# Seven half-depth products for eight in Q, K and the experts' first layers, and an accumulating transfer in the softmax sums, in a fused attention and expert kernel

## The chip, the cores and the metric

The kernel runs on one core of one Trainium2 chip. All data are fp32; only the negated row maxima of the softmax go through TensorE in bf16, each split into three bf16 parts. The metric is the device time of one execution in microseconds (us).

Engines are named as in the profile: PE is TensorE's matmul stream, PEld its weight loads, DVE is VectorE, ACT is ScalarE, POOL is GpSimd, SP is SyncE, which here only starts DMAs.

## The reference, cut to what matters

```python
xn = (x - mean(x)) / sqrt(var(x) + 1e-5)            # x: (4, 2048, 512)
q, k, v = split(xn @ qkv_w.T + qkv_b)               # 16 heads of 32
a = softmax(q @ k.T / sqrt(32)) @ v
attn = a @ proj_w.T + proj_b
idx = top_k(x_in[:, 0, :] @ Wr + br, 2)             # of 8 experts; x_in is xn's first token
h = gelu(xn @ W1[idx] + b1[idx])                    # 512 -> 512
ffn = sum(h @ W2[idx] + b2[idx]) / 2
out = x + attn + ffn
```

Each of the four batch entries ("batches" below) uses its own two experts, over all 2048 tokens.

## The kernel before, in words

**Units.** Attention is cut into *units*: one batch `b`, one group `g` of four heads (128 rows of Q and K), one chunk `qc` of 512 queries, one tile `kt` of 128 keys. 16 units make a chunk, 4 chunks a group, 4 groups a batch: 1024 units, written out by hand in one long loop over `U`, which starts 22 units early (`-LEAD`) because the row maxima run ahead of the softmax.

In each unit PE does four `shift` matmuls (minus the row maximum, L544), then `score` (L552) and `score_max` (L534, for a unit 22 later) in turns; ACT does four exponentials (L664) into a tile `p` (one for each head); DVE takes four maxima (L670). In every even unit PE also does `weigh` (L564: weights times V, of two units), and DVE adds the result to `sacc` (L573). POOL adds the unit's `p` tile to `psum` in `add_weights` (L581 and L583): the first of these in a chunk at `kt` 1, the last at `kt` 15 (the very last chunk of all has none). At `kt` 4 or 5 of the next chunk `add_keys` (L589) multiplies `psum` by ones to get the row sums; DVE inverts them in four pieces (L684) and POOL divides (L635).

**Items.** Every other product is an *item* placed in an odd unit, at most one to a unit, after its scores: a tile of Q or K (`kps`, `qps`), of V (`vps`), of an expert's first layer (`w1`, written as `hps`), of its second (`w2`, `ops`), or of the output projection (`prps`). An item is one PSUM bank of 128x512 and 16 calls of `nc.tensor.matmul`: four depth slices of 128, each as four column strips of 32 (L403). The trace has two instructions for a call, so an item is 32. Q, K and `w1` items leave PSUM by one ACT operation that adds the bias (L415), or by one on DVE (L413) where a gelu runs in the same unit; `w2` items by one DVE operation (L458) onto a `row` tile.

**The planner.** `Plan` gives every item its unit (the *slot*): Q, K and V at fixed places, the projection and the experts' items in the order of two queues in what is left. There are 534 slots, 496 items, 34 slots left empty ("rests", at `kt` 5). `Plan.loads` then says after which unit each tile is fetched: 8 units ahead of its first use, or when a buffer of its tag comes free. DMAs are all started on SP's queue, in program order; stores wait for a unit or two in `later`.

**Buffers.** PSUM has eight banks, all of one tag, taken in turn: a tile takes the bank of the tile eight before it. A unit takes eight banks for scores and maxima, a ninth for `weigh` or for an item; the ninth takes the bank of its own unit's first score tile. `p` has four buffers: the exponentials of unit `U+4` overwrite the tile of unit `U`, so they wait for everyone who reads that tile, POOL among them.

**Other work.** For the next batch, group 1 takes the statistics (DVE), group 2 normalizes (ACT) and transposes (`turn`: PE, copied by DVE); the results go to `xn_dram` and come back as `xq` or `xf`. POOL also adds the bias to 64 `row` tiles (L690).

Of the kernel before, what the change touches and what calls it, by code (L numbers as in the profile page):

```python
# [17 lines left out]
P = 128  # L18
# [3 lines left out]
TOP_K = 2  # L22
# [4 lines left out]
AHEAD = 6  # L27
WARN = 4


class Plan:
# [6 lines left out]
    def __init__(self, B, DC, NCH, NT, TPC):  # L38
# [11 lines left out]
        for t in range(NT):  # L50
            fixed[slots[t]] = ("v", 0, t)
        for G in range(1, B * DC):
            b, g = divmod(G, DC)
            for c in range(NCH):
                if g:
                    at = [(G - 1) * self.per_group + 2 * (7 + 4 * c) + 1]
                    todo = [("k", b, g, c), ("q", b, g, c)]
                else:
                    at = [(G - 2) * self.per_group + 2 * (27 + (2 + TPC) * c) + 1]
                    todo = [("k", b, g, c), ("q", b, g, c)]  # L60
                    todo += [("v", b, c * TPC + i) for i in range(TPC)]
                for n, item in enumerate(todo):
                    fixed[at[0] + 2 * n] = item
# [8 lines left out]
        for b in range(1, B):  # L72
            q1 = (b - 1) * self.per_seq + self.per_group
            q2 = q1 + self.per_group
            for n in range(NT):
                self.extra.setdefault(q1 + 2 * (16 + n) + 1, []).append(("stats", b, n))
                at = q2 + 2 * (1 + n + n // TPC) + 1
                self.extra.setdefault(at, []).append(("normal", b, n))
                self.extra.setdefault(at + 2, []).append(("turn", b, n))
            self.extra.setdefault(q2 + 1, []).append(("root", b, 0))  # L80
            for c in range(NCH):
                self.first_load[("xf", (b, c))] = self.first_load[("xq", (b, c))] = (
                    q2 + 2 * (2 + (TPC + 1) * c + TPC - 1) + 1 + 2
                )

        ffn = []
        for b in range(B):
            t0 = slots[0] if b == 0 else self.first_load[("xf", (b, 0))] + WARN
            order = list(range(NCH))
            if b == B - 1:  # L90
                order[NCH - 2 :] = order[: NCH - 3 : -1]
            for c in order:
                part = [("w1", b, c, k, f) for k in range(TOP_K) for f in range(DC)]
                part += [("w2", b, c, k, i) for k in range(TOP_K) for i in range(TPC)]
                ffn.append((t0, part))
# [16 lines left out]
        for s in slots:  # L112
            if s in fixed:
                self.items[s] = [fixed.pop(s)]
                before = None
                continue
            curve = before is not None and before[0] == "w1" and before[4] == DC - 1
            before = None
            if s in rests:
                owed += share  # L120
                if owed > 0 and not curve:
                    owed -= 1
                    continue
            if not current:
                for queue in (proj, ffn):
                    if queue and queue[0][0] <= s:
                        current = queue.pop(0)[1]
                        break
            if current:
                before = current.pop(0)  # L130
                self.items[s] = [before]
# [5 lines left out]

        for s in slots:
            for it in self.items.get(s, []):
                for tag, key in self.needs(it):  # L140
                    self.uses.append((s, tag, key))
            for kind, b, n in self.extra.get(s, []):
                if kind in ("stats", "normal"):
                    self.uses.append((s, "xl", (kind, b, n // TPC)))
                elif kind == "turn":
                    self.uses.append((s, "xq", ("stage", b, n // TPC)))
# [9 lines left out]
    @staticmethod  # L156
    def needs(item):
        TPC = CH // P
        kind, b = item[:2]
        if kind in "kq":  # L160
            g, c = item[2:]
            return [("xq", (b, c)), ("w" + kind, g)]
        if kind == "v":
            return [("xq", (b, item[2] // TPC)), ("wb", ("v",))]
        if kind == "w1":
            c, k, f = item[2:]
            return [("xf", (b, c)), ("w1", (b, k, f))]
        if kind == "w2":
            c, k, i = item[2:]
            return [("wb", ("w2", b, k)), ("row", (b, c, i))]  # L170
        qc, i = item[2:]
        return [("xl", ("at", b, qc)), ("wb", ("proj",)), ("prow", (b, qc, i))]
# [22 lines left out]
def block_kernel(  # L195
# [44 lines left out]
    xn_dram, v_dram, att_dram, part_dram = {}, {}, {}, {}  # L240
    for b in range(B):
        for c in range(NCH):
            xn_dram[b, c] = tc.dram_tile([P, DC, CH], F32, name=f"xn_dram_{b}_{c}")
            v_dram[b, c] = tc.dram_tile([P, TPC, D], F32, name=f"v_dram_{b}_{c}")
            att_dram[b, c] = tc.dram_tile([P, DC, CH], F32, name=f"att_dram_{b}_{c}")
            for i in range(TPC):
                part_dram[b, c, i] = tc.dram_tile([P, D], F32, name=f"part_dram_{b}_{c}_{i}")


    BUFS = {"xq": 2, "xf": 1, "xl": 1, "wk": 1, "wq": 1, "v": 6, "w1": 4, "wb": 2, "row": 4,  # L250
            "prow": 2}
# [10 lines left out]

    def x_rows(b, c):
        return x[b, ts(c, CH), :].rearrange("(t p) d -> p t d", p=P)

    def load(tag, key):
        name = f"{tag}_" + "_".join(str(k) for k in (key if isinstance(key, tuple) else (key,)))
        shape = {"xq": [P, DC, CH], "xf": [P, DC, CH], "xl": [P, TPC, D], "wb": [P, DC, D],
                 "row": [P, D], "prow": [P, D]}.get(tag, [P, DC, P])
# [4 lines left out]
        if tag in ("xq", "xf"):  # L274
            nc.sync.dma_start(t, xn_dram[key])
        elif tag == "v":
            b, g, c = key
            nc.sync.dma_start(t, v_dram[b, c][:, :, ts(g, P)])
        elif tag == "xl" and key[0] == "at":
            nc.sync.dma_start(t, att_dram[key[1:]])  # L280
        elif tag == "xl":
            nc.sync.dma_start(t, x_rows(*key[1:]))
        elif tag in ("wq", "wk"):
            col = "qkv".index(tag[1]) * D + key * P
            nc.sync.dma_start(t, qkv_wT.rearrange("(c p) n -> p c n", p=P)[:, :, col : col + P])
        elif tag == "w1":
            b, k, f = key
            src = W1[ds(expert(b, k), 1)].rearrange("o (c p) f -> p (o c) f", p=P)
            nc.sync.dma_start(t, src[:, :, ts(f, P)])
# [7 lines left out]
        elif tag == "row":  # L297
            b, c, i = key
            nc.sync.dma_start(t, x[b, c * CH + i * P : c * CH + (i + 1) * P, :])
# [24 lines left out]
    for c, tag in enumerate(("xl", "xf", "h", "h")):  # L324
        t = stream.tile([P, TPC, D], F32, tag=tag, name=f"x_0_{c}", bufs=2 if tag == "h" else 1)
        x_first.append(t)
# [8 lines left out]
    for tag in ("wk", "wq"):  # L335
        load(tag, 0)
    nc.sync.dma_start(x_first[1], x_rows(0, 1))
    nc.sync.dma_start(bv_bc, v_b.to_broadcast([P, D]))
    for c in range(2, NCH):
        nc.sync.dma_start(x_first[c], x_rows(0, c))  # L340

# [92 lines left out]

    def dense(item, U, on_dve):
        kind, b = item[:2]
        tiles = [held[n] for n in plan.needs(item)]
        if kind in "kq":
            project_qk(kind, *item[1:], *tiles, on_dve=on_dve)
        elif kind == "v":  # L440
            project_v(*item[1:], *tiles, U)
        elif kind == "w1":
            c, k, f = item[2:]
            xn, w = tiles
            if f == 0:
                hT[k] = stream.tile([P, DC, CH], F32, tag="h", name=f"h_{b}_{c}_{k}", bufs=2)
            pp = bank(f"hps_{b}_{c}_{k}_{f}")
            product(pp, [(w[:, d, :], xn[:, d, :]) for d in range(DC)])
            with_bias(hT[k][:, f, :], pp, b1s[b, k][:, f : f + 1], on_dve)
            if f == DC - 1:  # L450
                at = U + 2 if U > 0 or U == -1 else U + 1
                curves[at] = hT[k]
        elif kind == "w2":
            c, k, i = item[2:]
            w, row = tiles
            pp = bank(f"ops_{b}_{c}_{k}_{i}")
            product(pp, [(hT[k][:, f, ts(i, P)], w[:, f, :]) for f in range(DC)])
            nc.vector.scalar_tensor_tensor(row, pp, 0.5, row, ALU.mult, ALU.add)  # L458
            if k == TOP_K - 1:
                later(U + 2, lambda: nc.sync.dma_start(part_dram[b, c, i], row))  # L460
# [42 lines left out]
    for c in range(NCH):  # L503
        xn = load("xq", ("stage", 0, c))
# [5 lines left out]
        for kind in "kq":  # L510
            project_qk(kind, 0, 0, c, xn, held["w" + kind, 0])
# [63 lines left out]
    def add_weights(u):  # L575
# [3 lines left out]
        if kt == 1:  # L579
            psums[b, g, qc] = pair.tile([P, GH, CH], F32, tag="psum", name=f"psum_{b}_{g}_{qc}")  # L580
            nc.gpsimd.tensor_tensor(psums[b, g, qc], pT[u - 1], pT[u], ALU.add)  # L581
        else:
# [56 lines left out]
    for s, tag, key in loads.get(-LEAD - 1, []):  # L639
        load(tag, key)  # L640
    sum_bias(*load_bias(0))
    row_ready = {}

    for U in range(-LEAD, plan.units):
# [59 lines left out]
        for step, sb, n in plan.extra.get(U, []):  # L704
            if step == "stats":
                if n == 0:
                    norms[sb] = stat_tiles(sb)
                stats(norms[sb][0], n, held["xl", ("stats", sb, n // TPC)][:, n % TPC, :])
            elif step == "root":
# [3 lines left out]
            else:  # L713
                c, i = divmod(n, TPC)
                xs = held["xq", ("stage", sb, c)]
# [11 lines left out]
        for s, tag, key in loads.get(U, []):  # L727
            t = load(tag, key)
            if tag == "row":
# [6 lines left out]
        for n, c in ((16, NCH - 1), (1, NCH - 2)):  # L736
            if U == plan.units - n:
                tags = ("xf", "xq") if c == NCH - 1 else ("xl", "xq")
                t, rows = (
                    stream.tile([P, TPC, D], F32, tag=tag, name=f"end_{tag}", bufs=BUFS[tag])  # L740
                    for tag in tags
# [81 lines left out]
```

## Time and profile before

| | |
|---|---|
| median of three runs | 5113.08 us (5110.4 to 5116.17) |
| the profiled execution | 5115.77 us, of which 5114.0 us from its first to its last instruction (the span) |
| PE busy | 5037.9 us, 99% |
| POOL busy | 4534.9 us, 89% |
| DVE busy | 3448.0 us, 67% |
| ACT busy | 2515.2 us, 49% |
| DMA | 342.30 MB, mean 67 GB/s; 19.5% of the 16 DMA engines' time |
| granted PE clock | 0.998 |

Busy time is the time in which at least one instruction of an engine runs. Matmuls overlap each other and their ends are modelled, so the mean length of one (595 ns in an item) isn't its share of PE's time: the chain of waits gives that, where 32 of them take 3.57 us. In a row of the costliest groups stand the line, the engine, the operation, output and inputs by tile name, the shape, the count, the busy time, the mean of one, and then the idle time of the engine ahead of them with what ended it.

### The profile page before, as it was taken

To read this page: it belongs to the slowest core of one execution; us is meant where nothing else is said; L and a number is where in the kernel's file an instruction comes from. 1 tells how busy PE (TensorE), PEld (TensorE's weight loads), DVE (VectorE), ACT (ScalarE), POOL (GpSimd) and SP (SyncE) were. 2 spreads that over 40 slices of the span, in tenths; PEclk is the share of its full clock that TensorE was granted. 3 is DMA by queue.
4 is the path that set the end of the run, shared out by engine and by line. 5 is a ranking of instruction groups with operands and counts; after the bars stand their busy time and mean duration, and the time that the engine had idled before them with its cause. 6 is when DMAs were issued, how large, how long until landed. Compare 5 with 4: busy or idle time off the path is not lost. (4 is left out here: it accounts for less than half of the span.)

```text
span 5114.0 us, 108163 instructions
## 1 busy us (share of the span) xinstructions
PE 5037.9 (99%) x46020; PEld 1763.7 (34%) x46020; DVE 3448.0 (67%) x5491; ACT 2515.2 (49%) x4576; POOL 4534.9 (89%) x1430
## 2 busy tenths in 40 slices
PE   8999999999999999999999999999999999999999
PEld 2333333333333333333333333333333333333332
DVE  5666676776676677766776667766667666666762
ACT  1455555444544545554445545554454455545453
POOL 0699998998999999989999999989999999999992
PEclk9999999999999999999999999999999999999999
DMA  4211112211222212211122121312012121111112
GB/s 165 69 49 51 57 65 91 77 53 40 67 70 78 77 55 73 95 64 46 63 89 72 49 79 59 100 67 85 32 51 85 57 98 34 48 62 33 47 37 87
DMA packets 221732, 342.30 MB, mean 67 GB/s; under 512 B 14396, under 2 KB 129084, under 8 KB 207040
## 3 DMA queue, kind: packets, MB, share of 16 engines
q1 hardware_dynamic: 221248, 335.38, 19.5%
q8 instruction: 361, 5.91, 0.5%
q14 instruction: 123, 1.01, 0.1%
HBM read 251.71 MB, written 83.62 MB: 66 GB/s over the span
## 5 line engine op out<-in xcount | busy, mean ns | idle before, releaser
L583 POOL TENSOR_TENSOR psum<-psum,p 128x2048 f32<-128x2048 f32 x882 | 4008.1, 4544 | 193.3 <-ACT p L664 152.7
L670 DVE TENSOR_REDUCE mx<-m 128x1 f32<-128x512 f32 x4096 | 2542.4, 683 | 1041.2 <-PE m L534 1040.6
L664 ACT ACTIVATE p<-s 128x512 f32<-128x512 f32 x4096 | 2117.1, 603 | 1817.2 <-PE m L534 1729.7
L552 PE MATMUL s<-qT,kT 32*128 32x512 f32 x8192 | 1917.1, 587 | 0.0
L534 PE MATMUL m<-kT,qT 32*128 32x512 f32 x8192 | 1900.1, 589 | 3.9 <-ACT h L415 2.4
L534 PEld LDWEIGHTS m<-kT,qT 32*128 32x128 f32 x8192 | 926.2, 184 | 317.0 <-issue 242.8
L564 PE MATMUL acc<-p,v 128*32 128x512 f32 x8192 | 989.6, 601 | 38.5 <-ACT p L664 38.5
L552 PEld LDWEIGHTS s<-qT,kT 32*128 32x128 f32 x8192 | 767.7, 185 | 22.6 <-issue 2.2
L564 PEld LDWEIGHTS acc<-p,v 128*32 128x32 f32 x8192 | 214.7, 109 | 737.8 <-ACT p L664 423.4
L403 PE MATMUL ops<-wb_w,h 128*32 128x512 f32 x4096 | 466.0, 595 | 0.9 <-ACT p L664 0.2
L403 PE MATMUL hps<-xf,w 128*32 128x512 f32 x4096 | 466.0, 595 | 0.8
L573 DVE TENSOR_TENSOR sacc<-acc,sacc 128x512 f32<-128x512 f32 x448 | 309.7, 691 | 149.2 <-PE acc L564 149.2
L544 PE MATMUL s<-negm,ones_b 32*128 32x512 bf16 x4096 | 404.8, 385 | 2.0 <-ACT p L664 1.8
L544 PEld LDWEIGHTS <-ones_b 32*128 32x128 bf16 x4096 | 103.0, 91 | 857.5 <-issue 857.5
L581 POOL TENSOR_TENSOR psum<-p,p 128x2048 f32<-128x2048 f32 x63 | 286.0, 4540 | 119.4 <-ACT p L664 119.4
L415 ACT ACTIVATE h<-hps,b 128x512 f32<-128x512 f32 x114 | 78.3, 687 | 354.6 <-PE hps L403 354.6
L684 DVE RECIPROCAL sums<-sums 128x128 f32<-128x128 f32 x252 | 237.3, 942 | 0.7 <-ACT sums L601 0.7
L403 PE MATMUL vps<-wb_v,xq 128*32 128x512 f32 x2048 | 233.0, 595 | 2.3 <-issue 2.1
L403 PEld LDWEIGHTS ops<-wb_w,h 128*32 128x32 f32 x4096 | 120.0, 109 | 308.4 <-issue 229.8
L403 PEld LDWEIGHTS hps<-xf,w 128*32 128x32 f32 x4096 | 120.0, 109 | 307.0 <-issue 232.1
L403 PE MATMUL kps<-xq,wk 128*32 128x512 f32 x1920 | 218.4, 595 | 0.3 <-ACT p L664 0.3
L403 PE MATMUL qps<-xq,wq 128*32 128x512 f32 x1920 | 218.4, 595 | 0.1
(89 smaller groups left out, 1711.7 us busy)
## 6 DMA issues: line engine op xcount, KB each, us to landing
xq<-xn_dram SPq DMA_DIRECT2D x64, 1024.0 KB, 5.7
w<-in_W_dram SPq DMA_DIRECT2D x128, 256.0 KB, 3.2
xn_dram<-xq_stage SPq DMA_DIRECT2D x16, 1024.0 KB, 5.8
v_dram<-v SPq DMA_DIRECT2D x64, 256.0 KB, 2.6
xf<-xn_dram SPq DMA_DIRECT2D x16, 1024.0 KB, 5.5
v<-v_dram SPq DMA_DIRECT2D x64, 256.0 KB, 3.6
wb_w<-in_W_dram SPq DMA_DIRECT2D x16, 1024.0 KB, 6.6
row<-in_x_dram SPq DMA_DIRECT2D x64, 256.0 KB, 5.4
```

The costliest lines, as they stand in the source:

```text
L403: nc.tensor.matmul(pp[rows_of(j), :], lhsT[:, rows_of(j)], rhs, start=(first and n == 0), stop=(last and n == len(terms) - 1),)
L415: nc.scalar.activation(dst, src, AF.Identity, bias=col)
L534: nc.tensor.matmul(t, qT[b, g, qc][r, ts(i, P)], kT[b, g, kc][r, :], start=True, stop=True)
L544: nc.tensor.matmul(tiles[j], ones_b[r, :], negm[b, g, qc][r, :], start=True, stop=False)
L552: nc.tensor.matmul(tiles[j], kT[b, g, kt // TPC][r, ts(kt % TPC, P)], qT[b, g, qc][r, :], start=False, stop=True,)
L564: nc.tensor.matmul(acc[r, :], held["v", (b, g, kt // TPC)][:, (kt + n) % TPC, r], pT[u + n][:, j, :], start=(n == 0), stop=(n == 1),)
L573: nc.vector.tensor_tensor(t, acc, t, ALU.add)
L581: nc.gpsimd.tensor_tensor(psums[b, g, qc], pT[u - 1], pT[u], ALU.add)
L583: nc.gpsimd.tensor_tensor(psums[b, g, qc], psums[b, g, qc], pT[u], ALU.add)
L664: nc.scalar.activation(pT[U][:, j, :], tiles[j], AF.Exp, scale=SCALE)
L670: nc.vector.tensor_reduce(dst, t, AX.X, ALU.max, negate=True)
L684: nc.vector.reciprocal(sums[before][:, q], sums[before][:, q])
```

## The change

**Seven products.** Take a product of 2x2 blocks, C = A B, where A has two row blocks (K and Q of one group, or two 128-wide blocks of an expert's first layer) and two depth halves of 256, and B has two depth halves and two token chunks of 512. The kernel before forms the four blocks of C from eight half-depth products (two to an item). The kernel after forms seven:

```
S1 = A21 + A22    S2 = S1 - A11    S3 = A11 - A21    S4 = A12 - S2
T1 = B12 - B11    T2 = B22 - T1    T3 = B22 - B12    T4 = B21 - T2
P1 = A11 B11   P2 = A12 B21   P3 = S4 B22   P4 = A22 T4   P5 = S1 T1   P6 = S2 T2   P7 = S3 T3
C11 = P1 + P2                 C12 = P1 + P6 + P5 + P3
C21 = P1 + P6 + P7 + P4       C22 = P1 + P6 + P7 + P5
```

- The products of one step `i` for two blocks of the same kind (two pairs of chunks for Q and K, two pairs of rows for `w1`) share a slot: two banks, eight calls of matmul each. Steps go in the order 1, 6, 7, 5, 3, 4, 2, and step 5 is split over two slots of one product each, so that 8 slots stay 8. V, `w2` and the projection are as before.
- Every product is added into the SBUF tiles of C by `combine`: P1 is copied by ACT (or DVE), each of the others is added by one DVE operation, P5 by two.
- The weight sums S are made on POOL in place: for Q and K once at the start, for each expert in four operations of 128x512 (`ws`). The token sums T are made on POOL for each pair of chunks in four operations of 128x1024 in four units running (`tx`). Sums go to DRAM (`wqk_dram`, `ws_dram`, `t_dram`), and every product fetches its two factors as tiles `wt` (128 or 256 KB) and `xt` (512 KB).
- Experts' items now go by pair of chunks and by expert, so the `row` of the first expert is stored and fetched again for the second. Q's and K's slots move: the eight of a group stand in units 23 to 39 of the group before it (step 5 at `kt` 13 and 15).
- The tokens of batch 0 stay in `p` buffers until V is done. `v` has 4 buffers and not 6.

**The accumulating transfer.** The addition of a chunk's last `p` tile (`kt` 15) to `psum` is not a POOL operation any more but a DMA that adds, started on POOL's queue.

The core of the diff (loads, the list of uses and the tail are left out, except for what is told above):

```diff
+STEPS = (1, 6, 7, 5, 3, 4, 2)
+STORED = 6
...
+        halves = [(i, h) for i in STEPS for h in (((0,), (1,)) if i == 5 else ((0, 1),))]
         for G in range(1, B * DC):
             b, g = divmod(G, DC)
...
+            first = (G - 1) * self.per_group
+            for n, (i, h) in enumerate(halves):
+                at = (11, 12, 13, 14, 15, 16, 17, 19) if g else (3, 4, 5, 6, 7, 8, 9, 11)
+                fixed[first + 2 * at[n] + 1] = ("qk", b, g, i, h)
...
+            for k in range(TOP_K):
+                at = q1 + 2 * ((3 if b == 1 else 63) + 5 * k) + 1
+                for n in range(4):
+                    self.extra.setdefault(at + n, []).append(("ws", b, (k, n)))
...
+            for p in range(NCH // 2):
+                at = q2 + 2 * (12 + 15 * p) + 1
+                for n in range(4):
+                    self.extra.setdefault(at + n, []).append(("tx", b, (p, n)))
...
+                for k in range(TOP_K):
+                    part = [("w1", b, p, k, i, h) for i, h in halves]
+                    part += [("w2", b, p, 2 * p + 1, k, i) for i in range(TPC)]
+                    rest = [("w2", b, p, 2 * p, k, i) for i in range(TPC)]
+                    ffn += [(t0, part), (t0, rest)] if b == B - 1 else [(t0, part + rest)]
...
-    BUFS = {"xq": 2, "xf": 1, "xl": 1, "wk": 1, "wq": 1, "v": 6, "w1": 4, "wb": 2, "row": 4,
-            "prow": 2}
+    BUFS = {"xq": 2, "xt": 4, "xl": 1, "wt": 4, "v": 4, "wb": 2, "row": 4, "prow": 2}
...
+    def combine(i, x, c, b1, b2, on_dve):
+
+        add = nc.vector.tensor_tensor
+        biased = nc.vector.scalar_tensor_tensor
+        if i == 1 and on_dve:
+            nc.vector.tensor_copy(c[0, 0], x)
+        elif i == 1:
+            nc.scalar.activation(c[0, 0], x, AF.Identity)
+        elif i == 6:
+            add(c[0, 1], x, c[0, 0], ALU.add)
+        elif i == 7:
+            add(c[1, 0], x, c[0, 1], ALU.add)
+        elif i == 5:
+            biased(c[1, 1], x, b2, c[1, 0], ALU.add, ALU.add)
+            add(c[0, 1], x, c[0, 1], ALU.add)
+        else:
+            at, b_ = {3: ((0, 1), b1), 4: ((1, 0), b2), 2: ((0, 0), b1)}[i]
+            biased(c[at], x, b_, c[at], ALU.add, ALU.add)
...
+    def token_blocks(t, n):
+
+        sub = nc.gpsimd.tensor_tensor
+        b11, b12, b21, b22 = t[0][:, :2], t[1][:, :2], t[0][:, 2:], t[1][:, 2:]
+        if n == 0:
+            sub(b11, b12, b11, ALU.subtract)
+        elif n == 1:
+            sub(b12, b22, b12, ALU.subtract)
+        elif n == 2:
+            sub(b22, b22, b11, ALU.subtract)
+        else:
+            sub(b21, b21, b22, ALU.subtract)
...
-        if kind in "kq":
-            project_qk(kind, *item[1:], *tiles, on_dve=on_dve)
+        if kind == "qk":
+            g, i, pairs = item[2:]
+            for p, xt in zip(pairs, tiles[1:]):
+                pp = bank(f"qkps_{b}_{g}_{i}_{p}")
+                product(pp, [(tiles[0][:, d, 0, :], xt[:, d, :]) for d in range(2)])
...
+                combine(i, pp, o, bqkv[:, DC + g : DC + g + 1], bqkv[:, g : g + 1], on_dve)
...
+            for q in pairs:
+                pp = bank(f"hps_{b}_{p}_{k}_{i}_{q}")
+                product(pp, [(wt[:, d, q, :], xt[:, d, :]) for d in range(2)])
+                o = {(r, cc): hT[cc][:, 2 * q + r, :] for r in range(2) for cc in hT}
+                cols = [b1s[b, k][:, 2 * q + r : 2 * q + r + 1] for r in range(2)]
+                combine(i, pp, o, *cols, on_dve)
...
             nc.gpsimd.tensor_tensor(psums[b, g, qc], pT[u - 1], pT[u], ALU.add)
+        elif kt == NT - 1:
+            nc.gpsimd.dma_start(psums[b, g, qc], pT[u], accum_op=ALU.add)
         else:
             nc.gpsimd.tensor_tensor(psums[b, g, qc], psums[b, g, qc], pT[u], ALU.add)
...
+    for n in range(4):
+        weight_blocks(blocks_, n)
```

`weight_blocks` is built like `token_blocks`, over S1, S3, S2, S4.

## The prediction

> **What bounds the kernel now.** I read the page's busy line first, then the table of stages, then the chain of waits near the end for the price of each kind of PE work, then the timelines of the other engines.
>
> ```profile
> PE 5037.9 (99%) x46020; PEld 1763.7 (34%) x46020; DVE 3448.0 (67%) x5491; ACT 2515.2 (49%) x4576; POOL 4534.9 (89%) x1430
> 170.00:1000.00 830.00, 819.12 (x7520) 290.22 (x7512) 571.10 (x914) 436.36 (x782) 776.89 (x246) 1.00 0.18 59
> 1000.00:2000.00 1000.00, 993.38 (x9180) 347.42 (x9172) 692.50 (x1105) 492.66 (x910) 931.32 (x285) 1.00 0.19 64
> 4000.00:5000.00 1000.00, 989.97 (x9136) 345.78 (x9128) 671.61 (x1060) 509.98 (x925) 942.41 (x292) 1.00 0.16 52
> PE acc L564 <- ACT p L664: 38.5, 38, 1.4
> ACT p L664 <- POOL psum L583: 33.0, 16, 3.6
> ```
>
> In the stages (span, then PE, PEld, DVE, ACT and POOL busy) PE is full from 170 to 5000 us: the five stages I cut hold 4784.8 us of PE in 4830, so 45 us are idle, and 38.5 of these are waits of `acc` for an exponential. PE sets the time, and what leaves its stream leaves the span, unless another engine takes over. The nearest is POOL: 4504 us in the same 4830, 93%. It made ACT wait 16 times.
>
> ```profile
> 5022.24 2.58 PE keys L589 x24
> 5026.00 3.57 PE prps L403 x32
> 5030.75 1.85 PE acc L564 x16
> ```
>
> In the chain of waits (start, length) a full item of 32 instructions takes 3.57 us and `acc`, 16 of the same shape, 1.85. So 16 instructions cost 1.72, and 0.13 is paid once for a change of kind. [...]
>
> ```profile
> 2544.78 18.41 POOL L583 TENSOR_TENSOR psum<-psum,p 128x2048 f32<-128x2048 f32 x4
> 2564.73 4.54 POOL L581 TENSOR_TENSOR psum<-p,p 128x2048 f32<-128x2048 f32 x1 [1.54 <-ACT p L664]
> 2558.68 2.07 ACT L664 ACTIVATE p<-s 128x512 f32<-128x512 f32 x4 [3.55 <-PE m L534]
> 2562.58 2.07 ACT L664 ACTIVATE p<-s 128x512 f32<-128x512 f32 x4 [1.83 <-PE m L534]
> 2568.20 2.06 ACT L664 ACTIVATE p<-s 128x512 f32<-128x512 f32 x4 [3.55 <-PE m L534]
> 2572.09 2.07 ACT L664 ACTIVATE p<-s 128x512 f32<-128x512 f32 x4 [1.83 <-PE m L534]
> ```
>
> This is one chunk's end in the timelines of POOL and ACT. The four additions are `kt` 12 to 15, so the last starts near 2558.6. The exponentials are those of `kt` 0 to 3 of the next chunk; those at 2572.09 overwrite the tile of `kt` 15. Between the two lie 13.5 us, of which the addition uses 4.54. Read in this way, the 63 chunks give 10.0 to 19.7 us, median 13.9, with one exception: 4.6 in the last, where few items slow PE down. This **allowance** is the number to watch.
>
> **What the Trainium skill says.** Perfetto Trace Analysis, "Identifying the Most-Contended Engine", warns that matmul busy time is no measure of nearness to the roofline. The trace agrees as to lengths (595 ns against 3.57/32 = 112), which is why I price by the chain. DMA: Bandwidth & Descriptors, "Anatomy of one DMA — SWDGE (gpsimd) path", gives about 2.0 us plus bytes/436e3 for a POOL-started DMA. No such DMA is in this trace; SP's of 1 MB land in 5.2 to 7.7 us (medians). Collectives: The Full Stack, "The bandwidth ceiling: the fold count and why AG ≠ RS ≠ AR", says that a DMA that adds reads two sources for one write and so runs at half the rate of a copy; no run here shows it. SBUF — State Buffer, "Who interferes with whom", says that a DVE instruction with at most one SBUF input, outside the two-port modes, doesn't contend with GpSimd. The rows `row<-ops,row` and `sacc<-acc,sacc` are of that kind (one input in PSUM), and POOL's addition keeps to 4521 to 4576 ns through all of them. The new combining operations have the same form, so I charge POOL nothing for them.
>
> **The change, part by part.**
>
> *PE.* Step 5 stands in two slots with half an item each: 15 groups x 2, and 4 batches x 2 pairs x 2 experts x 2, are 62 half items; every other slot keeps 32 instructions. 62 x 1.72 = **106.6 us** leave PE (992 instructions). The 0.13 at a change of kind stays, since the slots remain 534 with 496 used. A second product within a slot changes only the bank; between `kps` and `qps`, which do that at the start, I see no gap. Nothing is added on PE.
>
> *DVE and ACT.* 15 x 2 + 16 x 2 = 62 sets of seven products need 434 DVE operations at 691 ns (row `row<-ops,row`), 300 us, and 62 ACT copies of 0.69. About 230 ACT operations of 0.69 (160 us) and 14 of DVE go. DVE comes to about 3740 of 5010, 75%. Per two units:
>
> ```profile
> 2520.22 2.48 DVE L670 TENSOR_REDUCE mx<-m 128x1 f32<-128x512 f32 x4 [0.47 <-PE m L534]
> 2526.78 0.94 DVE L684 RECIPROCAL sums<-sums 128x128 f32<-128x128 f32 x1
> 2528.58 0.69 DVE L458 SCALAR_TENSOR_TENSOR row<-ops,row 128x512 f32<-128x512 f32 x1 [0.86 <-PE ops L403]
> 2529.74 2.48 DVE L670 TENSOR_REDUCE mx<-m 128x1 f32<-128x512 f32 x4 [0.47 <-PE m L534]
> ```
>
> In 9.52 us DVE does 2 x 2.48 + 0.69 (`sacc`) + 0.94 + 0.69 = 7.3. With a full item of two products the first sum fits into the 0.86 of waiting, and the second ends where today's only one does: 0 us. With a half item the pair takes 7.8 on PE, and DVE needs 7.0 without and 8.0 with an inversion; it comes 0.2 to 0.9 us late to the next maxima. The bank that needs them soonest is taken about 1 us later, so that is absorbed. Where statistics (0.84 an odd unit) or copies of transposes fall on a half item it isn't. Bounds 0 and 62 x 0.7 = 43; I take 5. The new bank wait, the second product's for its own unit's second score tile, is met: that exponential is done some 1.2 us before.
>
> *POOL.* 63 additions of 4.544 go (286 us). Added: 32 operations of 128x1024 for tokens at 2.36 (between the rows of 1.27 for 512 and 4.54 for 2048), 76 us; 32 of 128x512 for experts, 41; four for Q and K, 9, in the start, where POOL is idle; 63 DMA starts of about 1 us, the skill's first-byte figure, 63. The net is -97. POOL in all is no bound, but a burst is. The four token operations of a pair stand in four units running: 9.5 us of work where POOL gains some 0.2 a unit, so it is about **8.4 us later** from there to the chunk's end. Six such bursts lie in the loop (two for each later batch; batch 0's are in the start).
>
> *The accumulating transfer.* It waits on POOL's queue for the addition of `kt` 14. Behind it stands only the next chunk's `kt` 1, which waits for ACT anyway. `add_keys` comes some 23 us later. The wait that matters is the exponentials' for the `p` tile. Its length T, from POOL's start to landing, is unknown. Low: skill, two reads, 2.0 + 2 x 2.4 = 6.8. High: a plain 1 MB transfer of the trace (5.7) with three passes of its moving part, 2.0 + 3 x 3.7 = 13. I take 8.5, the low value plus descriptor work and other traffic. Against the allowances, less 8.4 in the six bursts, less 3.4 in the 15 chunks whose end has both halves of step 5 (PE comes 2 x 1.72 earlier), less 4.2 for four expert bursts: three bursts are left with 2.1 to 3.9, three with 4.7 to 4.8, and cost 28 us; the last chunk costs 4; expert bursts 2; all others nothing. Sum **35 us**, straight onto PE, since in `kt` 3 the item's bank is the first exponential's. (T = 6.8 gives 21, 10 gives 52.)
>
> *DMA and SP.* I count some 590 more starts on SP at 0.38 us each (median of its 797 recorded now): 7% becomes 11% of its time. About 170 MB of loads and stores come in, and 66 MB of additions, on 342: 19.5% of DMA time becomes 30 to 35%. The start runs at 56% already. Products' tiles come at least four units (over 15 us) before use and land in 4 to 6: hidden by PE's own stream; bound 0 to 20 us, I take 0. Start and tail keep their order: 0, within 3 either way.
>
> *Sum.* 5115.8 (the profiled execution) - 106.6 + 35 + 5 = 5049. The median of the runs is 2.7 lower, so 5047.
>
> **The rivals.**
> - *Full gain* (0.19). T is under 6, or bursts are eaten by slack: 5113 - 107 + 5 = 5011; 5000 to 5020. For it: in mid-chunk `p` tiles have about 10 us of slack. Against it: those 10 are what a burst takes.
> - *DVE or loads take over* (0.10). Half items are paid at the high bound, 43, and loads come late for 10: 5113 - 107 + 35 + 53 = 5094; 5075 to 5103. For it: statistics and copies fill DVE in stretches. Against it: its largest wait today is for PE, 1041 us.
> - *The transfer is slow* (0.13 slower, 0.05 about even). With T = 12.6 the same sum is 107 and eats the whole gain; beyond that all 63 chunk ends lose time, and at 14 it is 156: 5113 - 107 + 156 + 5 = 5167. For it: nothing in the trace bounds an adding DMA. Against it: it needs 1.5 times what I take.
> - *The work doesn't fall.* If the compiled program had as many matmuls, nothing would move; the diff gives seven products in each set, so I give this no share.
>
> **How the numbers follow.** The likeliest case, 5020 to 5075 around 5047, has 0.53. From 5004 to 5100 I take in it, most of the full gain and most of the third: 0.8. A measurement here can tell about 0.2% (10 us) from no change: faster 0.82, same 0.05, slower 0.13.
>
> **What would show it.** Right: PE down to 45,028 instructions, idle between 170 us and the end up from 45 us to some 85; ACT waits for a DMA into `psum`, worst behind token sums; DVE near 3740, POOL near 4440. Wrong: such waits at most chunk ends (T over 12), none (under 6), or matmuls `m` and `s` waiting for DVE.

## The result: 0.5% slower, and where the time went

Median of six runs 5139.97 us (5135.2 to 5141.35) against 5113.4 us for the kernel before (six runs, 5110.4 to 5116.17): ratio 1.0050, interval 1.0037 to 1.0063. The forecast was 5047. The profiled execution took 5141.04 us, with a span of 5139.3.

First the page's busy line, the stages (span, then PE, PEld, DVE, ACT and POOL busy, PE clock, share of DMA, GB/s), three rows of the waits (us in total, times, longest) and the row of the transfer's issues:

```profile
PE 4999.0 (97%) x45028; PEld 1738.2 (34%) x45028; DVE 3723.4 (72%) x5911; ACT 2392.9 (47%) x4404; POOL 4426.3 (86%) x1498
170.00:1000.00 830.00, 803.33 (x7232) 280.79 (x7228) 619.81 (x985) 409.35 (x739) 751.59 (x257) 0.99 0.36 112
1000.00:2000.00 1000.00, 987.04 (x9000) 343.80 (x8989) 748.69 (x1193) 472.34 (x883) 898.15 (x290) 1.00 0.35 106
4000.00:5000.00 1000.00, 989.21 (x9028) 343.38 (x9020) 745.52 (x1174) 488.79 (x898) 901.11 (x294) 1.00 0.32 94
ACT p L836 <- DMA psum<-p: 76.6, 10, 12.3
ACT p L836 <- POOL psum L753: 50.9, 17, 3.9
PE acc L732 <- ACT p L836: 37.3, 37, 1.2
psum<-p POOLq DMA_DIRECT2D x63, 1024.0 KB, 8.0
```

The work fell as it should: 45,028 matmul instructions, 992 fewer. But PE is busy for 4999 us and not for 5037.9 - 106.6 = 4931. So some 68 us are lost inside groups of matmuls, to stalls or to a slower clock, where the idle time of a row doesn't show them. A new wait, ACT for the DMA into `psum`, came ten times and lasted up to 12.3 us.

To find both I cut the trace into units, at the start of each `shift`, and took from each the kinds of work in it (`shift`, `s` and `m` 1.94, `acc` 1.86, a full item 3.57, a half one 1.86, the rarer kinds likewise, and 0.11 between units). What is left of a unit is its **excess**, which is negative where the units are shorter than this sum:

| excess, us | before | after |
|---|---|---|
| even units behind a half item (60 in the loop) | 0 | 56.1 |
| units of `kt` 3, behind a chunk's end | 0 | 63.3 |
| the last chunk | -10.9 | -4.7 |
| all others | 53.8 | 60.4 |
| sum | 42.9 | 175.1 |

132.2 more, less the 106.6 saved, is 25.6; the span grew by 25.3. The two large rows are to be explained.

*Combinations* are POOL's operations that form S and T; a *burst* is the four of one pair of chunks (token burst) or of one expert (expert burst). Here is the end of chunk 9, which has a token burst, in the timelines of POOL, ACT and PE (start, length):

```profile
933.77 4.58 POOL L753 TENSOR_TENSOR psum<-psum,p 128x2048 f32<-128x2048 f32 x1
938.66 0.87 POOL L751 DMA_DIRECT2D psum<-p  x1 [0.30 <-POOL psum L753]
939.27 4.80 POOL L749 TENSOR_TENSOR psum<-p,p 128x2048 f32<-128x2048 f32 x1
938.39 2.07 ACT L836 ACTIVATE p<-s 128x512 f32<-128x512 f32 x4 [2.98 <-POOL psum L753]
950.39 2.06 ACT L836 ACTIVATE p<-s 128x512 f32<-128x512 f32 x4 [9.93 <-DMA psum<-p]
942.42 0.59 PE L720 MATMUL s<-qT,kT 32*128 32x512 f32 x2
951.04 1.12 PE L449 MATMUL xt<-ident,xl_normal 128*128 128x128 f32 x4 [8.04 <-ACT p L836]
952.09 4.68 PE L479 MATMUL qkps<-xt,wt_qk 128*32 128x512 f32 x32
```

The transfer starts at 938.66, 13.2 us after the exponentials of its tile; this *lag* is 4.0 in the median chunk. The exponentials of the next `kt` 3 wait for it until 950.39, 11.7 us later. PE stands for 8.04. Then its full item takes 4.68 instead of 3.57, for the clock is halved from 947.4 to 954.2. At the end of the program the same is in the chain of waits; the kernel before has no such wait there:

```profile
5029.91 12.08 DMA psum<-p
5042.09 0.60 ACT p L836
...
5045.03 2.75 PE acc L732 x16
...
5051.54 3.57 PE prps L479 x32
5056.29 1.85 PE acc L732 x16
```

The last transfer is on the path for 12.08 us, and the `acc` behind it took 2.75 instead of 1.85 (half clock again). The undisturbed prices, 3.57 and 1.85, are those of before.

A half item and the even unit behind it, in the timelines of DVE and PE:

```profile
4337.37 0.75 DVE L524 SCALAR_TENSOR_TENSOR qT<-qkps,bqkv,qT 128x512 f32<-128x512 f32 x1 [0.29 <-PE qkps L479]
4338.04 0.68 DVE L525 TENSOR_TENSOR kT<-qkps,kT 128x512 f32<-128x512 f32 x1
4338.63 2.47 DVE L842 TENSOR_REDUCE mx<-m 128x1 f32<-128x512 f32 x4
4337.23 0.40 PE L712 MATMUL s<-negm,ones_b 32*128 32x512 bf16 x4
4338.86 1.09 PE L702 MATMUL m<-kT,qT 32*128 32x512 f32 x2
4339.89 1.92 PE L732 MATMUL acc<-p,v 128*32 128x512 f32 x16
```

The unit starts at 4337.23. DVE does step 5's two operations one after the other; L525 ends at 4338.72, and the last `m` starts at 4338.86. `acc` comes 2.66 us after the unit's start. The product's bank is the last that its unit takes, and counted from there the last `m` of the next unit is the eighth tile: it takes this very bank. In all 60 of these units the trace shows the last `m` starting 0.15 us after the end of L525, which itself ends 1.5 to 2.8 us after the unit's start in all but two.

**Theories.** A: at the chunk ends it is the transfer's place in POOL's queue, behind bursts of combinations, that makes it late. Rivals: the transfer costs at every chunk end, or other DMAs delay it. B: behind half items it is the bank, held through two DVE operations. Rival: DVE simply has too much to do there.

### The profile page after: what moved, and what is told of

It reads as the page before. It is cut to its first block, busy times and chain, and to the rows that moved or that the text cites. A ratio compares the mean times of both kernels' runs of the same rounds, so it can differ in the third digit from the quotient of the medians.

```text
span 5139.3 us, 107890 instructions
## 1 busy us (share of the span) xinstructions
PE 4999.0 (97%) x45028; PEld 1738.2 (34%) x45028; DVE 3723.4 (72%) x5911; ACT 2392.9 (47%) x4404; POOL 4426.3 (86%) x1498
## 5 line engine op out<-in xcount | busy, mean ns | idle before, releaser
L753 POOL TENSOR_TENSOR psum<-psum,p 128x2048 f32<-128x2048 f32 x819 | 3721.7, 4544 | 221.9 <-ACT p L836 186.0
L702 PE MATMUL m<-kT,qT 32*128 32x512 f32 x8192 | 1951.8, 590 | 10.6 <-DVE h L525 5.7
L479 PE MATMUL hps<-xt,wt_w 128*32 128x512 f32 x3584 | 412.4, 597 | 13.2 <-ACT p L836 12.6
L479 PE MATMUL qkps<-xt,wt_qk 128*32 128x512 f32 x3360 | 392.3, 605 | 19.5 <-ACT p L836 19.0
L620 DVE SCALAR_TENSOR_TENSOR row<-ops,row 128x512 f32<-128x512 f32 x128 | 88.4, 691 | 173.8 <-PE ops L479 115.3
L479 PE MATMUL prps<-wb_proj,xl_at 128*32 128x512 f32 x1792 | 203.9, 595 | 0.3
L479 PEld LDWEIGHTS hps<-xt,wt_w 128*32 128x32 f32 x3584 | 103.6, 110 | 282.0 <-issue 187.5
L479 PEld LDWEIGHTS qkps<-xt,wt_qk 128*32 128x32 f32 x3360 | 97.9, 111 | 284.7 <-issue 184.3
```

Source lines behind the costliest of these rows:

```text
L479: nc.tensor.matmul(pp[rows_of(j), :], lhsT[:, rows_of(j)], rhs, start=(first and n == 0), stop=(last and n == len(terms) - 1),)
L702: nc.tensor.matmul(t, qT[b, g, qc][r, ts(i, P)], kT[b, g, kc][r, :], start=True, stop=True)
L753: nc.gpsimd.tensor_tensor(psums[b, g, qc], psums[b, g, qc], pT[u], ALU.add)
```

## The experiments

Times are medians, ratios stand against the kernel before, with their interval. Line numbers shift by a few between kernels.

### One part undone: no transfer

```diff
-        elif kt == NT - 1:
-            nc.gpsimd.dma_start(psums[b, g, qc], pT[u], accum_op=ALU.add)
```

> The changed kernel (5140) with the accumulating transfer undone: the addition of kt 15 is again made by POOL. Two theories. A: the loss sits at chunk ends where POOL's queue is some 13 us behind and the transfer then takes 8 to 14 us, so that kt 3 of the next chunk waits (about 69 us in ten chunks) and TensorE's clock halves after such waits. B: the loss sits in the 62 half items, whose bank VectorE gives back only after two operations (about 40 us). By A the same ten chunk ends now need 4.5 us instead of 8 to 14, but POOL gets 63 x (4.54 - 0.87) = 231 us more work, 4658 in all (91%): 5080 to 5115. If instead POOL is what is short and the transfer relieved it: over 5150. By B alone, with the chunk ends costing little: within 10 us of 5140. The units after the 62 half items stay 0.5 to 1 us too long by both.

Measured: 5086.12 us, 0.9943 (0.9929 to 0.9956). The page's busy line, and the waits for `psum`:

```profile
PE 4988.6 (98%) x45028; PEld 1736.4 (34%) x45028; DVE 3724.9 (73%) x5911; ACT 2392.4 (47%) x4404; POOL 4657.6 (92%) x1498
ACT p L834 <- POOL psum L751: 78.5, 23, 4.7
```

The excess of `kt` 3 fell from 63.3 to 3.2, that behind half items stayed (61.8). With POOL at 92%, ACT waits for its additions 23 times, but never for more than 4.7 us. So the seven products alone are faster than eight, and the transfer in the place of POOL's addition costs 54 us.

### The transfer alone, in the kernel before

```diff
+        elif kt == NT - 1:
+            nc.gpsimd.dma_start(psums[b, g, qc], pT[u], accum_op=ALU.add)
```

> The kernel before (5113) with one part of the change alone: the addition of kt 15 by an accumulating transfer in place of POOL's operation. It has no token or expert combinations on POOL and less DMA traffic, and its chunk ends have an allowance of 10.0 to 19.7 us, median 13.9, against a transfer of about 8.0. By theory A (the transfer costs only where a burst of combinations stands ahead of it): no difference, 5105 to 5125, with waits of ACT for a DMA into psum under 15 us in all; POOL falls by 231 us to about 4304. If the transfer itself is what costs, at all chunk ends: 5150 or more.

Measured: 5127.73 us, 1.0029 (1.0019 to 1.0040); `kt` 3 has an excess of 1.2 in all.

```profile
ACT p L666 <- DMA psum<-p: 12.5, 2, 10.5
ACT p L666 <- POOL psum L585: 44.0, 16, 3.6
```

There are two waits for the DMA, one of them 10.5: that of the last chunk, whose excess rose by 10.9. The 62 others cost next to nothing, though the transfer's median is 7.9 us here too and the longest takes 13.8. "At all chunk ends" falls. The time is 3 us above the expected range: the last chunk's 11 us are not in the expectation.

### The combinations on VectorE

```diff
     def token_blocks(t, n):
-        sub = nc.gpsimd.tensor_tensor
+        sub = nc.vector.tensor_tensor
```

`weight_blocks` likewise, except for Q's and K's weights in the start.

> The changed kernel with the 28 token and 12 or so expert combinations of the loop moved from POOL to VectorE, at the same places of the program; transfers, loads and stores stay. POOL loses over 100 us and its four-operation bursts; VectorE gets 60 or so operations of about 1.1 us. By theory A (POOL's lag ahead of the transfer): the waits of ACT for the DMA into psum fall from 77 to under 25 us, the time to 5070 to 5095. If the transfer is late because other DMAs (the stores of the combined tiles, the loads) are ahead of it, not because of POOL: the waits stay over 50 us and the time over 5120. By B the half items' 40 us remain in either case.

Measured: 5189.63 us, 1.0146 (1.0131 to 1.0162). The expected time was missed, but not by theory A: `kt` 3's excess is 2.0, and ACT's waits for the transfer are 10.5 us in two, for 76.6 in ten. The loss is a new one, in units where the combinations run. Two rows of the groups by shape, the same line seven times, six of them in the loop, and once in the start, where POOL is idle:

```profile
L548 DVE TENSOR_TENSOR xq_stage<-xq_stage,xq_stage 128x1024 f32<-128x1024 f32 x7 | 20.3, 2900 | 0.0
L548 DVE TENSOR_TENSOR stage<-stage,stage 128x1024 f32<-128x1024 f32 x1 | 1.2, 1217 | 0.0
```

2900 ns instead of 1217. My 1.1 us held for an idle POOL alone.

### Step 5 from SBUF

```diff
-            biased(c[1, 1], x, b2, c[1, 0], ALU.add, ALU.add)
-            add(c[0, 1], x, c[0, 1], ALU.add)
+            nc.scalar.activation(c[1, 1], x, AF.Identity, bias=b2)
+            biased(c[0, 1], c[1, 1], b2, c[0, 1], ALU.subtract, ALU.add)
+            add(c[1, 1], c[1, 1], c[1, 0], ALU.add)
```

> The changed kernel with only step 5's combination rewritten: ACT reads the product's bank once (copy with the bias), and VectorE makes both sums from SBUF, so that the bank is free after one ACT operation of some 0.69 us instead of two VectorE operations of 0.75 and 0.68 that run one after the other. The number of VectorE operations stays, ACT gets 62 more (43 us). By theory B (the last m of the unit after a half item waits for this bank) the units after half items go from 4.5 to 4.9 us back to about 3.9: 40 us less in all, 5095 to 5110. If VectorE is late with the maxima themselves, and not the bank: under 10 us less. If ACT's extra operation delays the next exponentials instead: 5140 or more.

Measured: 5326.31 us, 1.0414 (1.0400 to 1.0428), far slower than expected. DVE's and POOL's timelines, and a row by shape:

```profile
617.76 1.69 DVE L525 SCALAR_TENSOR_TENSOR kT<-qT,bqkv,kT 128x512 f32<-128x512 f32 x1 [0.20 <-ACT qT L524]
619.49 4.89 DVE L526 TENSOR_TENSOR qT<-qT,qT 128x512 f32<-128x512 f32 x1
614.36 9.47 POOL L754 TENSOR_TENSOR psum<-psum,p 128x2048 f32<-128x2048 f32 x2
L526 DVE TENSOR_TENSOR h<-h,h 128x512 f32<-128x512 f32 x32 | 95.0, 2969 | 1.1
```

The operation of 0.69 us takes 4.89: it ends at 624.38, 0.55 after POOL's second addition (623.83). So do all 86 of the 124 that took over 1 us: 546 to 561 ns after the end of a POOL operation. The Trainium skill, SBUF — State Buffer, "Who interferes with whom", says that a DVE instruction with two SBUF inputs contends with a GpSimd instruction that reads SBUF; here it waited for the whole operation. The change's own DVE operations, with one input in PSUM, keep to 0.62 to 0.75. On theory B this run says little: with the bank given back by one ACT operation no excess (0.1) is left in the even units behind half items, as B has it, but the slow operations cost far more in the units after them.

### The last m later

```diff
...
+            if half and h == 1:
+                for dst, t in maxima:
+                    nc.vector.tensor_reduce(dst, t, AX.X, ALU.max, negate=True)
+                maxima.clear()
+                weigh(U - 2)
             if first_pass is not None:
                 score_max(first_pass, (2 - 2 * h, 3 - 2 * h), maxima)
...
```

`half` holds in the even unit behind a half item; the later call of `weigh` is left out there.

> The changed kernel (5140) with one change of order: in the even unit behind a half item, acc and its sum into sacc come ahead of the second pair of m, not behind it. No operation is added or dropped; the two operations of step 5 stay on VectorE and read the product's bank. The m that takes this bank is then issued some 2.8 us after the unit's start instead of some 1.1. By theory B (the last m waits for the bank, which comes free about 1.6 us after the unit's start): the units after half items lose their 56 us of excess but for a few, and the time is 5080 to 5095. If VectorE is simply too busy behind a half item, the same work only waits elsewhere: over 5125. The waits for the transfer (63 us of excess in the units of kt 3, 8 at the end) stay by both.

Measured: 5161.36 us, 1.0092 (1.0077 to 1.0108): 21 us slower than the change. PE and DVE behind the same half item as above:

```profile
4355.13 0.70 PE L702 MATMUL m<-kT,qT 32*128 32x512 f32 x2
4355.27 0.69 DVE L741 TENSOR_TENSOR sacc<-acc,sacc 128x512 f32<-128x512 f32 x1 [1.35 <-PE acc L732]
4356.29 3.68 DVE L849 TENSOR_REDUCE mx<-m 128x1 f32<-128x512 f32 x6 [0.33 <-PE m L702]
```

The even unit now keeps its length (3.9 us from 4351.24), as theory B has it: the 60 have an excess of some 2 us in all. But the two late `m` no longer run beside `s`; DVE first idles 1.35, then has six maxima in a row, and the next unit takes 5.39 instead of 3.9. The next units have some 88 us of excess in all, so the time lies where the expectation puts the rival. That the new order made this wait, and not a lack of DVE time, is a reading of this timeline; the other split and the other dealing below part the two.

Two kernels were built on this order, one without the transfer and one with it in 52 chunks:

> Both losses taken away: the later m behind half items, and POOL's addition in place of the accumulating transfer. If the two theories together are the whole loss, the savings add: 5086 (the transfer alone undone) less 50 to 56, so 5030 to 5040, which is the kernel before less nearly all of the 107 us of matmuls. If a third loss is left or POOL, now with 4658 us of work in a shorter span, becomes the bound: over 5055.

> As the kernel with the later m, but the accumulating transfer is kept in 52 of the 63 chunks and undone in the 11 (5, 9, 11, 24, 25, 27, 28, 41, 43, 44 and 62) in which a burst of combinations or the program's end makes it late. POOL keeps most of its relief (about 4466 us). By theory A the transfer costs nothing in the 52, and it lets POOL work off what the bursts leave: 5015 to 5035, and no more than the kernel without any transfer. If a transfer costs a little in every chunk: above the kernel without transfers.

Measured: 5107.24 (0.9987; 0.9981 to 0.9994) and 5107.10 (0.9985; 0.9978 to 0.9991). Both stand 21 above the kernel without the transfer, as this one does above the change: they repeat the loss of the order.

### Another step split

```diff
-        halves = [(i, h) for i in STEPS for h in (((0,), (1,)) if i == 5 else ((0, 1),))]
+        halves = [(i, h) for i in STEPS for h in (((0,), (1,)) if i == 4 else ((0, 1),))]
...
```

What is left out moves some slots of Q, K and V in the first group of a batch.

> The changed kernel with step 4 in two slots instead of step 5 (and the slots of the first group of a batch moved by one so that the Q tiles come free in time; the V items of that group come one slot later). Half items then need one VectorE operation, and the 31 slots of step 5 are full, with two operations behind each of their two products. By theory B only the last product of those 31 slots gives its bank back late, so the excess is about halved: 28 us less, 5105 to 5120. If it is the half item's shortness (VectorE late with the maxima) that costs, nothing is won: 5135 to 5145.

Measured: 5126.14 us, 1.0026 (1.0017 to 1.0036), 14 less than the change, half of the saving expected. But the saving isn't the expected one. Behind half items with one operation, and no gelu, the excess is 0.23 a unit (10.5 over 46) where it was 0.94; behind the full slots of step 5 it is 0.68 each (21.2 over 31). But in 16 of the experts' half slots a gelu now runs on ACT, and behind those it is 3.0 each (48.3), where a gelu in a full slot costs 1.22. These rows hold 80 us, and their like in the change 76 (56.1 and 16 gelus of 1.22), so nothing was won there. The 14 us come from `kt` 3, whose excess fell from 63.3 to 48.5; this was not forecast, and why it fell was not tested. The single rows still say something of theory B: what counts is the number of operations behind a slot's last product, not the half item as such, for a full slot that ends with two pays too. And a half item is a bad place for a gelu.

### Seven products dealt out otherwise

```diff
+        halves = [[(1, both)], [(6, both)], [(7, (0,))], [(7, (1,))], [(5, (0,)), (3, (0,))],
+                  [(5, (1,)), (3, (1,))], [(4, both)], [(2, both)]]
...
```

What is left out lets a slot hold two items, and starts a gelu behind the second half of step 3.

> The changed kernel (5140) with the seven products dealt out otherwise over the same eight slots: steps 1, 6, 4 and 2 full, step 7 in two half slots, and steps 5 and 3 together in two full slots, each holding step 5 and then step 3 of one pair. So no slot ends with step 5: what ends last in a slot has one VectorE operation behind it, and no half item stands where a gelu runs. Matmuls, VectorE operations, loads and transfers stay as they are. By theory B (two VectorE operations in a row behind the last product of a slot keep its bank from the last m): the 56 us of excess behind half items fall to about 10 (the kernel with step 4 split showed 0.15 each behind half items with one operation), so 5090 to 5098; the 63 us of kt 3 and the 8 at the end stay. If it is the half item's shortness itself: 5130 or more. If loads for two steps in one slot come late: above 5110, with TensorE waiting for DMA.

Measured: 5129.94 us, 1.0032 (1.0020 to 1.0044). DVE and PE at a slot of steps 5 and 3, and the wait for the transfer:

```profile
4336.27 0.68 DVE L529 TENSOR_TENSOR kT<-qkps,kT 128x512 f32<-128x512 f32 x1
4337.32 0.75 DVE L532 SCALAR_TENSOR_TENSOR kT<-qkps,bqkv,kT 128x512 f32<-128x512 f32 x1 [0.37 <-PE qkps L483]
4338.55 2.48 DVE L846 TENSOR_REDUCE mx<-m 128x1 f32<-128x512 f32 x4 [0.48 <-PE m L706]
4337.19 0.40 PE L716 MATMUL s<-negm,ones_b 32*128 32x512 bf16 x4
4339.23 1.92 PE L736 MATMUL acc<-p,v 128*32 128x512 f32 x16
ACT p L840 <- DMA psum<-p: 92.3, 14, 11.8
```

Step 5's second operation (L529) is done before the slot ends, one is left behind it, and `acc` comes 2.04 us after the unit's start instead of 2.66. Behind half items 19.5 us are left of 56.1. Behind the slots that hold step 5 there are only some 4 us, though DVE has three operations in each and as many in all as in the change. So theory B holds for the mechanism. But the time fell by 10 and not by 45: `kt` 3 rose from 63.3 to 75.2, with 14 waits for the transfer instead of ten, and the rest rose by 16. With PE faster the lag grew: at the end of chunk 9 it is 15.2 us and not 13.2.

### The same without the transfer, and with it in 52 chunks

> As the kernel dealt out otherwise, with POOL's addition in place of the accumulating transfer. By A and B together the two savings add: 5086 less some 46, so 5035 to 5045, faster than the kernel before by 1.3 to 1.5%, and only 15 to 20 us of the excess that the kernel before doesn't have are left (POOL behind bursts). If another loss hides behind these two: over 5060.

Measured: 5063.84 us, 0.9901 (0.9886 to 0.9916), the fastest whole kernel of the study. Busy line and one stage:

```profile
PE 4965.3 (98%) x45028; PEld 1736.1 (34%) x45028; DVE 3728.9 (74%) x5911; ACT 2392.0 (47%) x4404; POOL 4656.9 (92%) x1498
1000.00:2000.00 1000.00, 990.01 (x9056) 345.60 (x9048) 757.85 (x1201) 481.05 (x893) 949.93 (x293) 1.00 0.29 94
```

The saving behind half items is whole (61.8 to 19.9), but half of it comes back elsewhere: 22 us less than without the transfer alone, where 46 were expected. POOL is busy for 95% of this stage.

> As the kernel dealt out otherwise, with the transfer kept in 52 chunks and undone in the 11 (5, 9, 11, 24, 25, 27, 28, 41, 43, 44 and 62) with a burst or the program's end. By theory A a transfer in an undisturbed chunk costs nothing, and POOL (4466 us of work instead of 4658) works off what a burst leaves a little sooner: equal to the kernel with no transfer or up to 10 us less. If each transfer costs a little: more.

Measured: 5067.22 us, 0.9908 (0.9893 to 0.9923): 3 us more than without any, and the same within both intervals. Transfers kept where they were expected to do no harm bring nothing, though POOL has 190 us less to do.

### No bursts

```diff
-            token_blocks(pair_, n)
+            if b == 0:
+                token_blocks(pair_, n)
```

`weight_blocks` likewise. This kernel leaves the combinations of batches 1 to 3 out, so their products are formed from blocks that are not combined; it is for the time alone.

> As the kernel dealt out otherwise with all its transfers (5130), but the 24 token and 24 expert combinations of batches 1 to 3 are left out; their tiles are loaded, stored and read as before, uncombined. So POOL has no bursts in the loop, while the accumulating transfers and every other DMA stay. By theory A (what makes the transfer late is POOL's place in its queue): the 75 us of excess in the units of kt 3 fall to under 5, only the last chunk's 8 stay, and the time is 5040 to 5060, no more than with the transfer undone (5064). If the transfer is late for the other DMAs at those chunk ends (token stores and loads): over 40 us stay and the time is above 5095.

Measured: 5048.32 us, 0.9871 (0.9854 to 0.9887), 82 us less than with them. Chunk 9's end in POOL's timeline, and the wait:

```profile
913.31 4.56 POOL L759 TENSOR_TENSOR psum<-psum,p 128x2048 f32<-128x2048 f32 x1
918.16 0.87 POOL L757 DMA_DIRECT2D psum<-p  x1 [0.30 <-POOL psum L759]
921.48 4.55 POOL L755 TENSOR_TENSOR psum<-p,p 128x2048 f32<-128x2048 f32 x1 [2.45 <-ACT p L842]
ACT p L842 <- DMA psum<-p: 18.5, 4, 9.4
```

The transfer now starts 6.3 us after its exponentials instead of 15.2, POOL waits for ACT again, and the excess of `kt` 3 is 5.7 instead of 75.2. Every other DMA is there, and the slowest transfer still takes 13.1 us. So the bursts in POOL's queue make the loss; the other DMAs alone do not. This doesn't clear them wholly: chunk 9's transfer, started sooner, also took less time here, 7.9 us and not 10.4. The one long wait left (9.4) is the last chunk's.

## Why the prediction was wrong

The forecast took 5 us for the half items and 35 for the transfer; they cost 56 and 69.5. These two terms make up 86 of the 93 us between 5047 and 5140.

- **PE, right.** 106.6 us of matmuls left, at 1.72 a half item; a second product in a slot costs no more.
- **DVE, wrong by the largest ratio: 5 us taken, 56 measured.** The failing sentence is "The bank that needs them soonest is taken about 1 us later, so that is absorbed". It asks when DVE is done with the maxima's banks and leaves out the product's own, which the last `m` of the next unit takes. With two operations in a row it comes free 1.49 us after that unit's start (4338.72 - 4337.23), and 0.6 to 1.9 us of PE are lost each time but for two with more. The upper bound, 62 x 0.7 = 43, was too low as well.
- **The transfer, right in kind, 35 us taken and 69.5 measured** (63.3 and, in the last chunk, 6.2). T has a median of 8.0 for my 8.5. The low value was 6.8, from the two source reads that the Trainium skill gives for the add of a collective (Collectives: The Full Stack, "The bandwidth ceiling: the fold count and why AG ≠ RS ≠ AR"); the fastest took 6.9, so the trace agrees with it where little else moves. POOL's lag was 9.2 us more in token chunks, for my 8.4, which is near. Mis-sized was that one T served for all: the six token chunks had 7.9 to 11.6. With these in the place of 8.5 the prediction's own allowances give 39 us (an estimate); the six cost 41.8, not 28. The expert bursts, for which I took 2, cost some 20, most of it in chunk 28, where POOL came 9 us later than in the median chunk, for the 4.2 taken, and the transfer took 14.0. The last chunk cost 6, not 4.
- **Why some transfers are long.** It isn't the lag: chunk 38's, with a lag of 1.1, took 12.3 and cost nothing, and with the combinations on VectorE chunk 9's took 10.7 with a lag of 0.5. The length goes with what other transfers move meanwhile: on the mean some 0.4 MB beside the 45 transfers under 9 us, and 1.7 MB beside the 16 over 10. Chunks 9 and 11 had the same lag of 13.2; beside the first one's transfer 1.46 MB moved and it took 11.6, beside the second's 0.71 and it took 8.6, and their `kt` 3 lost 9.6 and 3.7. So lag and traffic both enter the wait. No run changed the traffic alone.
- **The clock, not in the list.** Long waits of PE are followed by half clock: 61 us of it for 10 before (up to 5060 us). With PE at work, a half-clock microsecond loses half a microsecond, so at most 25 us of the two rows are this.
- **POOL and DMA, right.** POOL 4426 for 4440; 29.0% of DMA time on the hardware queues and 6.5% on POOL's for 30 to 35; no load took over. A start of the transfer took 0.87 us of POOL; the prediction's 1 us is a first-byte latency, which is another thing. The rival "DVE or loads take over" was right as to DVE, with 43 for the half items and 35 for the transfer; it was 56 and 69.5, and the loads it held for 10 cost nothing. "The transfer is slow" was not it: ten waits, not most of the chunk ends.

In the best whole kernel some 57 of the 107 us are still missing: by its excess 20 behind half items and 37 in other units. ACT waits 75.9 us for POOL in all, 33.0 before. What share of that the bursts have without any transfer was not tried.

## What to carry to other kernels

Count banks from the tile that is written last: in a ring of eight, the last operation that reads it sets when the eighth tile after it starts, and one more operation in a row there is paid at every slot. An asynchronous transfer is issued from a queue; price it from the time when the queue gets to it, with the length that it has beside the other transfers of that stretch, in the worst stretch and not the median one. And look whether the engine that it frees was short of time at all. When the bounding engine gets faster, the next engine's slack shrinks, so two fixes are measured together and not only apart.

## What the runs showed of the hardware

- An adding DMA of 1 MB, SBUF to SBUF in fp32, took 6.9 to 14.0 us from POOL's start to landing, median 8.0, and 0.87 of POOL itself. The 16 over 10 us had some 1.7 MB of other transfers beside them, the 45 under 9 us some 0.4.
- A DVE operation with both inputs in SBUF can wait for POOL's running operation: 86 of 124 took over 1 us and ended 0.55 us after one of POOL, the longest in 5.0 us instead of 0.69.
- PE at half clock comes in pieces of 3.4 us: one to three in a row behind the longer waits, so an `acc` of 1.85 took 2.75. The Trainium skill, TensorE: Matmul & The Clock Gate, "Part 1: The HAM clock gate (the "warmup" mystery)", tells of two states, half and full, and of windows of about 3.4 us; this trace agrees in both.
